# Queries of the second cross-attention by seven block products, around the output projection

## The chip, the cores and the metric

The kernel runs on one NeuronCore of one Trainium2 chip. The metric is the device time of one execution in microseconds (us); a lower time is better. The engines are called PE (TensorE, matrix products; its weight loads are shown as PEld), DVE (VectorE), ACT (ScalarE), POOL (GpSimd) and SP (SyncE, which here only issues transfers).

## The reference, cut to what matters

A decoder of two layers works on 8 sequences of 256 tokens with 256 features, all in float32. Each layer has self-attention, cross-attention and an expert stage, each with a residual sum. The change lies in the cross-attention of the second layer, 16 heads of 64:

```python
q = _split_heads(jnp.einsum('bnd,df->bnf', x, Wq))        # x: 8 x 256 x 256 after a layer norm, Wq: 256 x 1024
kv = jnp.einsum('bmc,cf->bmf', context, Wkv)              # context: 8 x 256 x 512, Wkv: 512 x 2048
k, v = jnp.split(kv, 2, axis=-1)
...                                                        # a null key and value are put in front
sim = jnp.einsum('bhid,bhjd->bhij', q * scale, k)
out = jnp.einsum('bhij,bhjd->bhid', jax.nn.softmax(sim, axis=-1), v)
out = jnp.einsum('bnf,fd->bnd', out, Wout)                 # Wout: 1024 x 256
out = (out - mu) * jax.lax.rsqrt(var + EPS) * ln_scale + ln_bias
```

## The kernel before

The program is traced in Python and then put in order by a planner: for each engine it chooses the order of the instructions by the order of the source and by when its own model of the chip has each one ready. An engine then runs its instructions strictly in that order, and an instruction whose inputs are not ready holds up all behind it. In a region marked `manual_schedule(engines={PE})` the instructions of PE keep the order of the source among themselves; where instructions from outside the region fall between them, and the order on the other engines, stay the planner's.

The stage is `null_cross_attention` (line 1057). It loops over the 8 sequences b (line 1359; called rounds here). A round has these steps:

1. `context(b + 1)` issues the load of the next sequence's context from SP into ctxT (512 KB, two buffers in the pool `ctxs`, line 765).
2. `weighted` (1220): for each of 8 chunks of two heads the scores `stx` from qT and kT, their exponential on ACT (`pTx`), the sum of both key halves on POOL (`both`), the products with the values (`ox`) and the denominators (`den`). In this part PE's order is the planner's.
3. `layernorm_T(b + 1)` (262): the next sequence's rows are normalized on DVE into `xn`, transposed on PE (`tr`, line 283) and copied by ACT into `xnT`. Both tiles have two buffers.
4. `sums_of_context` (1105): four sums of blocks of ctxT on DVE, for step 6.
5. From b = 1 on, `routed_norm(b - 1)` and `routed_rows` (958, 968) do the same as step 3 with the finished rows of sequence b - 1, for the router (tile `xne`, in the buffers of `xn`).
6. From here PE's order is that of the source. Keys and values of sequence b + 1 are made by `seven` (1121): the product of a 2 x 2 block matrix with a 2 x 2 block matrix by seven block products instead of eight. `seven` is a generator, and each `next` makes one step of it:

- step 1: product 1 into bank x; ACT copies the bank (p).
- step 2: product 2 into bank z, and DVE adds p: block (0,0) of the result. Product 5 into bank y; ACT copies it (v).
- step 3: product 6 onto bank x; ACT copies it (u).
- step 4: product 7 onto bank x; DVE adds v: block (1,1).
- step 5: product 3 onto bank y; DVE adds u: block (0,1). Then product 4 onto bank x; ACT copies it: block (1,0).

The first index of a block is the half of the tokens, the second the half of the features. In the program's names the products write `kv` and `kvz`. The sums of weight blocks are made once, ahead of the loop (`sums_of_weights`, 1094).
7. `reciprocals` (1283) of the denominators go through memory (rd, rs on SP) and POOL multiplies them into oT (`divide`, 1315).
8. `routed_scores(b - 1)` (971): the router's scores, small products into `sc`.
9. `queries` (1205): first the null key's scores (`nps`, ACT exponentiates them into `en`), and behind step 10 the queries of sequence b + 1, `fm`, by `feature` (1062): eight products of half a block each, 64 matmul records in 4 PSUM tiles, which DVE copies into qT.
10. `outward` (1321): the output projection `wo`, a copy by ACT, statistics on DVE, a power on POOL, normalized rows on DVE, scale and bias on POOL, and the residual sum on POOL.

The order in which PE gets steps 6, 8, 9 and 10 is written out by hand:

```python
for made in (k7, k7, v7, k7, k7, v7, v7):
    next(made)
if b:
    routed_scores(b - 1)
next(q)
next(v7)
next(v7)
...
divide(oT, rs, (nc.gpsimd, nc.gpsimd if more else nc.vector))
outward(b, oT, old)
if more:
    *_, (qT, en) = q
```

The queries of sequence 0 are made ahead of the loop; the last round makes none. PSUM has three tiles of the kind `mm` (one bank), two of the kind `sc` (two banks: `stx`, and the banks x and y of `seven`) and one for the denominators.

Of the kernel before, what the change touches and what calls it, by code (L numbers as in the profile page):

```python
# [155 lines left out]
def plain(  # L156
# [105 lines left out]
    def layernorm_T(b, work, mm):  # L262

        xn = work.tile([P, 2, D], F32, tag="xn", name="xn")
        mv, rs = norm_stats([x[:, 2 * b + t, :] for t in range(2)], 1e-5, small, "ln")
        for t in range(2):
            last = normed(xn[:, t, :], x[:, 2 * b + t, :], mv, rs, t)
        return last, transposed(xn, work, mm, "xnT")
# [9 lines left out]
    def transposed(rows, work, mm, tag, dst=None):  # L278

        ps = mm.tile([P, 2, 2 * P], F32, tag="mm", name="tr")  # L280
        for t in range(2):
            for c in range(2):
                nc.tensor.transpose(ps[:, c, t * P : (t + 1) * P], rows[:, t, c * P : (c + 1) * P], ident)  # L283
        if dst is None:
            dst = work.tile([P, 2, 2 * P], F32, tag=tag, name=tag)
        nc.scalar.copy(dst, ps)  # L286
        return dst
# [472 lines left out]
    def weights_x():  # L760

        w_exp.close()
        wd = ctx.enter_context(tc.tile_pool(name="wd", bufs=1, side="right"))
        wproj = ExitStack()
        ctxs = wproj.enter_context(tc.tile_pool(name="ctxs", bufs=2, side="right"))
        wp = wproj.enter_context(tc.tile_pool(name="wp", bufs=1, side="right"))
        wkv_x = wp.tile([P, CTX // P, 2 * XH * XD], F32, name="wkv_x")
        wq_x = wp.tile([P, 2, XH * XD], F32, name="wq_x")
        wout_x = wd.tile([P, XH * XD // P, D], F32, name="wout_x")
        nc.gpsimd.dma_start(wkv_x, a["L1_xattn_Wkv"].rearrange("(c p) f -> p c f", p=P))  # L770
        nc.gpsimd.dma_start(wq_x, a["L1_xattn_Wq"].rearrange("(c p) f -> p c f", p=P))
        nc.gpsimd.dma_start(wout_x, a["L1_xattn_Wout"].rearrange("(c p) f -> p c f", p=P))
        nkv = a["L1_xattn_null_kv"]
        nkrow = wd.tile([P, XD], F32, name="nkrow")
        nc.sync.dma_start(nkrow, nkv[0:1, :].to_broadcast([P, XD]))
        nvcol = wd.tile([P, 1], F32, name="nvcol")
        for g in range(2):
            nc.sync.dma_start(nvcol[XD * g : XD * (g + 1), :], nkv[1:2, :].rearrange("o d -> d o"))
        lns = wd.tile([P, D], F32, name="lns")
        nc.sync.dma_start(lns, a["L1_xattn_ln_scale"].rearrange("(o d) -> o d", o=1).to_broadcast([P, D]))  # L780
        lnb = wd.tile([P, D], F32, name="lnb")
        nc.sync.dma_start(lnb, a["L1_xattn_ln_bias"].rearrange("(o d) -> o d", o=1).to_broadcast([P, D]))
        return wd, ctxs, wproj, wkv_x, wq_x, wout_x, nkrow, nvcol, lns, lnb
# [174 lines left out]
    def routed_norm(b, work):  # L958

        xn = work.tile([P, 2, D], F32, tag="xn", name="xne")  # L960
        mv, rs = norm_stats([x[:, 2 * b + t, :] for t in range(2)], 1e-5, small, "ln")
        for kept, v in zip(norms[b], (mv, rs)):
            nc.gpsimd.tensor_copy(kept, v)
        for t in range(2):
            normed(xn[:, t, :], x[:, 2 * b + t, :], mv, rs, t)
        return xn
# [90 lines left out]
    def null_cross_attention(phase):  # L1057
# [4 lines left out]
        def feature(dst, w, rows, copy, c2):  # L1062

            n = w.shape[1]
            ps = mm.tile([P, 2, S], F32, tag="mm", name="fm")
            for i in range(2):
                for cc in range(n):
                    product(ps[:, i, :], w[:, cc, (c2 + i) * P : (c2 + i + 1) * P], rows[:, cc, :], cc == 0, cc == n - 1)
            copy(dst[:, c2 : c2 + 2, :], ps)

        def features(dst, w, rows, copy):
            for c2 in range(0, nc8, 2):
                feature(dst, w, rows, copy, c2)
# [6 lines left out]
        def keys(ctxT):  # L1080
            kT = work.tile([P, nc8, S], F32, tag="kT", name="kTx", bufs=1)
            features(kT, wkv_x, ctxT, nc.scalar.copy)
            return kT

        half = CTX // P // 2

        def w_block(j, k):

            return wkv_x.rearrange("p c (m k f) -> p c m k f", m=2, k=2)[:, half * j : half * (j + 1), :, k, :]

        tw = wsum.tile([P, 3, half, 2, XH * XD // 2], F32, name="tw")
        t1, t2, t3, t4 = tw[:, 0], tw[:, 1], w_block(0, 1), tw[:, 2]

        def sums_of_weights(n):
            dst, p, q = (
                (t1, w_block(0, 1), w_block(0, 0)),
                (t2, w_block(1, 1), t1),
                (t4, w_block(1, 0), t2),
                (t3, w_block(1, 1), w_block(0, 1)),
            )[n]  # L1100
            for m in range(2):
                for c in range(half):
                    nc.vector.tensor_tensor(dst[:, c, m], p[:, c, m], q[:, c, m], ALU.subtract)

        def sums_of_context(ctxT):


            def block(i, j):
                return ctxT[:, half * j : half * (j + 1), bass.ts(i, P)]

            sw = wsum.tile([P, 3, half, P], F32, tag="sw", name="sw")
            s1, s2, s3, s4 = sw[:, 0], sw[:, 1], block(1, 0), sw[:, 2]
# [6 lines left out]
        w_terms = w_block(0, 0), w_block(1, 0), w_block(1, 1), t4, t1, t2, t3  # L1119

        def seven(terms, m, dst):

            xy = scp.tile([P, 2, 2 * S], F32, tag="sc", name=f"kv{m}")
# [8 lines left out]
            def product_of(n, bank, fresh):  # L1132

                s, t = terms[n - 1], w_terms[n - 1][:, :, m, :]
                for i in range(4 if m == 0 else 1):
                    for c in range(half):
                        if m == 0:
                            args = bank[:, bass.ts(i, P)], t[:, c, bass.ts(i, P)], s[:, c, :]
                        else:
                            args = bank, s[:, c, :], t[:, c, :]  # L1140
                        for made in product(*args, fresh and i == 0 and c == 0, c == half - 1):
# [4 lines left out]
            if m == 0:  # L1146
# [7 lines left out]
            else:  # L1154

                def of(i, j):
                    return dst[:, i, 8 * j : 8 * j + 8, :]

                def seen(bank):
                    return bank.rearrange("p (h d) -> p h d", h=8)  # L1160

            def kept(bank, name):
                t = work.tile([P, 2 * S], F32, tag="pT", name=f"kv{name}{m}", bufs=4)
                reads(bank, nc.scalar.copy(t, bank))
                return seen(t)
# [4 lines left out]
            zb = mm.tile([P, 2 * S], F32, tag="mm", name=f"kvz{m}")  # L1170
# [12 lines left out]
            reads(yb, nc.vector.tensor_tensor(of(0, 1), u, seen(yb), ALU.add))  # L1183
            product_of(4, xb, False)
# [3 lines left out]
        def vals(ctxT):  # L1188
            v = work.tile([P, 2, XH, XD], F32, tag="vx", name="vx", bufs=1)
# [13 lines left out]
            return v  # L1203

        def queries(xnT):

# [5 lines left out]
            yield  # L1212
            qT = work.tile([P, nc8, S], F32, tag="qT", name="qTx", bufs=1)
            for c2 in range(0, nc8, 2):
                feature(qT, wq_x, xnT, nc.vector.tensor_copy, c2)
                if c2 == 0:
                    yield
            yield qT, en
# [102 lines left out]
        def outward(b, oT, en):  # L1321
# [9 lines left out]
            for t in range(2):  # L1331
                xt = x[:, 2 * b + t, :]
                normed(y[:, t, :], y[:, t, :], mv, rs, t)
                nc.gpsimd.tensor_tensor(y[:, t, :], y[:, t, :], lns, ALU.mult)
                nc.gpsimd.tensor_tensor(y[:, t, :], y[:, t, :], lnb, ALU.add)
# [11 lines left out]


        _, xnT = layernorm_T(0, work, mm)
        ctxT = context(0)  # L1350
        kT = keys(ctxT)
        for n in range(3):
            sums_of_weights(n)
        v = vals(ctxT)
        *_, (qT, en) = queries(xnT)
        sums_of_weights(3)
        load_router()
        order = ExitStack()
        for b in range(B):
# [4 lines left out]
            if more:  # L1364
                _, xnT = layernorm_T(b + 1, work, mm)
                terms = sums_of_context(ctxT)
# [10 lines left out]
            if more:  # L1377
                order.enter_context(tc.manual_schedule(engines={mybir.EngineType.PE}))
                kT = work.tile([P, nc8, S], F32, tag="kT", name="kTx", bufs=1)
                v = work.tile([P, 2, XH, XD], F32, tag="vx", name="vx", bufs=1)  # L1380
                k7, v7, q = seven(terms, 0, kT), seven(terms, 1, v), queries(xnT)
# [7 lines left out]
            if more:  # L1389

                for made in (k7, k7, v7, k7, k7, v7, v7):
                    next(made)
                if b:
                    routed_scores(b - 1)
                next(q)
                next(v7)
                next(v7)
# [5 lines left out]
            outward(b, oT, old)  # L1403
            if more:
                *_, (qT, en) = q
# [1231 lines left out]
```

## Time and profile before

| | us |
|---|---|
| median of 3 runs | 1377.46 |
| lowest and highest | 1375.84 to 1378.7 |
| the profiled execution | 1375.28 |
| its span in the profile | 1373.6 |

The span reaches from the first to the last instruction that the profile shows; the profiled execution's own time is 1.7 us longer. The granted clock of PE was 0.994 of full speed over the span. The stage of the change runs from 659 to about 1150 us. A float32 product appears in the trace as two records of MATMUL and two of LDWEIGHTS; `product` (272) makes two products of 64 columns each, so it stands for four records. The "mean ns" of a matmul record is its latency; records overlap, so a step is costed from its start to the start of the next.

### The profile page before, as it was taken

What the parts mean: (1) busy time and instruction counts of PE and PEld (TensorE: products, weight loads), DVE (VectorE), ACT (ScalarE), POOL (GpSimd) and SP (SyncE); (2) the same over time, 40 slices, a digit from 0 to 9 for tenths busy, and PEclk for the clock granted to TensorE, in tenths of its full rate; (3) what the DMA queues carried; (4) which work ended last, traced back from release to release, by engine and by line L of the source; (5) the groups of instructions that cost most, each with busy time, mean ns of one, the idle gap of its engine ahead of it and who ended that gap; (6) DMA issues with size and microseconds to landing.
All of it is one profiled execution on the core that took longest, in us unless ns stands there. A gap on an engine that the chain in (4) does not pass through costs nothing.

```text
span 1373.6 us, 30022 instructions
## 1 busy us (share of the span) xinstructions
PE 1333.9 (97%) x12814; PEld 902.7 (66%) x12814; DVE 533.9 (39%) x1539; ACT 457.2 (33%) x730; POOL 404.6 (29%) x513
## 2 busy tenths in 40 slices
PE   6999999999999999999999999999999999999998
PEld 3666756756766756764767566676756645788884
DVE  5443563463475555344233222232232236322223
ACT  2455443543543433531313223131322212022221
POOL 4322052051033243320334424152442512400004
PEclk9999999999999999999999999999999999999999
DMA  8960000000000004100011010101101111689954
GB/s 311 340 224 16 9 25 1 17 24 1 2 9 2 2 9 153 72 2 1 27 36 33 16 32 16 48 6 43 33 1 33 64 32 36 264 336 399 395 196 129
DMA packets 46926, 116.65 MB, mean 85 GB/s; under 512 B 8272, under 2 KB 30400, under 8 KB 42432
## 3 DMA queue, kind: packets, MB, share of 16 engines
q1 hardware_dynamic: 38912, 92.74, 19.7%
q0 software_dynamic: 5152, 18.89, 3.8%
q10 hardware_dynamic: 2720, 3.02, 0.6%
q8 instruction: 103, 1.69, 0.5%
q14 instruction: 39, 0.32, 0.1%
HBM read 104.00 MB, written 27.93 MB: 96 GB/s over the span
## 4 chain that ended last, share of the span: by engine, by line
PE 82%; DMA 6%; DVE 5%; POOL 3%; issue 1%; ACT 1%; SPq 1%; ACTq 0%; POOLq 0%; DVEq 0%
PE kv L274 11%; PE st L334 8%; PE o L366 8%; PE h L274 6%; PE fm L274 5%; PE wo L274 5%; PE ox L1266 4%; PE stx L1228 4%; PE out L1625 3%; PE out L1442 3%; PE h L952 3%; PE qk L274 3%; PE hx L952 3%; PE tr L283 2%; PE den L1242 2%; PE ao L274 2%
## 5 line engine op out<-in xcount | busy, mean ns | idle before, releaser
L366 PE MATMUL o<-pT,padv 128*64 128x256 f32 (+1 forms) x1536 | 171.6, 365 | 1.2 <-POOL pT L346 1.2
L343 ACT ACTIVATE pT<-st 128x1024 f32<-128x1024 f32 (+1 forms) x128 | 110.4, 915 | 88.2 <-PE st L334 87.4
L366 PEld LDWEIGHTS o<-pT,padv 128*64 128x64 f32 x1536 | 103.1, 137 | 52.7 <-issue 9.9
L334 PE MATMUL st<-qm,kT 64*128 64x256 f32 (+1 forms) x1024 | 116.3, 365 | 0.9 <-DVE qm L312 0.6
L334 PEld LDWEIGHTS st<-qm,kT 64*128 64x128 f32 x1024 | 89.2, 188 | 25.9 <-issue 15.6
L1234 POOL TENSOR_TENSOR both<-pTx 128x512 f32<-128x512 f32 x64 | 79.7, 1280 | 55.4 <-ACT pTx L1232 38.9
L1232 ACT ACTIVATE pTx<-stx 128x1024 f32<-128x1024 f32 x64 | 62.1, 1021 | 88.1 <-PE stx L1228 87.6
L274 PE MATMUL h<-xrT,w 128*64 128x128 f32 (+1 forms) x1936 | 87.0, 250 | 1.5 <-issue 1.5
L274 PEld LDWEIGHTS h<-xrT,w 128*64 128x64 f32 x1936 | 84.4, 137 | 4.3 <-issue 2.1
L256 POOL TENSOR_TENSOR lnrs<-lnve,mhalf 128x2 f32<-128x2 f32 x48 | 33.6, 701 | 150.9 <-DVE lnve L254 99.1
L343 ACT ACTIVATE pT<-st,kbias 128x1024 f32<-128x1024 f32 x64 | 68.0, 1113 | 28.7 <-PE st L334 28.7
L334 PE MATMUL st<-qm,memk 64*128 64x256 f32 x512 | 68.8, 393 | 0.5
L945 DVE TENSOR_TENSOR midr<-sl,h 128x128 f32<-128x128 f32 x102 | 29.4, 288 | 102.2 <-PE h L274 69.0
L944 ACT ACTIVATE sl<-h 128x128 f32<-128x128 f32 (+1 forms) x114 | 35.4, 310 | 96.2 <-PE h L274 56.7
L1228 PE MATMUL stx<-qTx,kTx 64*128 64x256 f32 x512 | 64.3, 391 | 2.5 <-ACT pTx L1232 2.5
L346 POOL TENSOR_SCALAR_AFFINE_SELECT pT<-pT 128x512 f32<-128x512 f32 x64 | 39.5, 638 | 83.2 <-ACT pT L343 80.0
L274 PE MATMUL qk<-l_wqkv,xnT 128*64 128x512 f32 x256 | 62.3, 608 | 0.7 <-ACT xnT L286 0.7
L1266 PE MATMUL ox<-pTx,vx 128*64 128x256 f32 x512 | 61.1, 381 | 0.0
L1228 PEld LDWEIGHTS stx<-qTx,kTx 64*128 64x128 f32 x512 | 46.1, 186 | 20.3 <-issue 9.2
L274 PE MATMUL wo<-wout_x,oT 128*64 128x256 f32 x512 | 58.0, 379 | 0.0
L334 PEld LDWEIGHTS st<-qm,memk 64*128 64x128 f32 x512 | 48.0, 186 | 15.1 <-issue 5.1
L274 PE MATMUL fm<-xnT,wq_x 128*64 128x256 f32 x512 | 57.0, 379 | 0.0
(312 smaller groups left out, 2204.2 us busy)
## 6 DMA issues: line engine op xcount, KB each, us to landing
w<-packs SPq DMA_DIRECT2D x22, 1408.0 KB
w<-packs SPq DMA_DIRECT2D x22, 768.0 KB
rs<-rd SPq DMA_DIRECT2D x16, 512.0 KB
packs<-L_ffn_w_eDF SPq DMA_DIRECT2D x8, 704.0 KB
packs<-L_ffn_w_eDF SPq DMA_DIRECT2D x8, 640.0 KB
packs<-L_ffn_w_eFD SPq DMA_DIRECT2D x8, 640.0 KB
ctxT<-ctx_T SPq DMA_DIRECT2D x8, 512.0 KB
wkv_x<-L_xattn_Wkv POOLq DMA_DIRECT2D x1, 4096.0 KB, 18.4
```

The costliest lines, as they stand in the source:

```text
L274: nc.tensor.matmul(out[h], lhsT[:, h], rhs, start=start, stop=stop, skip_group_check=True)
L334: nc.tensor.matmul(st[:, g, i, :n], kT[rows, c, bass.ts(kt, P)], qm[rows, 2 * mq + i, c, q0:], start=True, stop=True,)
L343: nc.scalar.activation(pT[:, :, :, :n], st[:, :, :, :n], AF.Exp, scale=scale, **kb)
L346: nc.gpsimd.affine_select(out=pT[:, :, :, :P], in_=pT[:, :, :, :P], compare_op=ALU.is_ge, fill=0.0, base=0, pattern=[[0, 2], [0, 2], [1, P ...
L366: nc.tensor.matmul(o[64 * i : 64 * i + 64, mq, q0:], v_pad[:, kt, 4 * c + 2 * mq + i, 2 * g : 2 * g + 2, :], pTs[kt][:, g, i, : S - q0], s ...
L952: nc.tensor.matmul(h, shared["ws13"][:, c, lo : lo + P], shared["xnT"][:, c, bass.ts(q, 2 * S)], start=c == 0, stop=c == 1)
L1228: nc.tensor.matmul(st[:, g, kt, :], kT[rows, c, bass.ts(kt, P)], qT[rows, c, :], start=True, stop=True)
L1232: nc.scalar.activation(pT, st, AF.Exp, scale=scale)
L1234: nc.gpsimd.tensor_tensor(both, pT[:, :, 0, :], pT[:, :, 1, :], ALU.add)
L1266: nc.tensor.matmul(o[XD * g : XD * (g + 1), i, :], v[:, kt, 2 * (c2 + i) + g, :], pT[:, g, kt, :], start=kt == 0, stop=kt == 1, skip_group ...
L1442: nc.tensor.matmul(ps, mid[:, i, lo : lo + P], w2[:, i, :], start=i == 0, stop=i == NFC - 1)
L1625: nc.tensor.matmul(ps[h], mid[:, i, h], sets[k % len(sets)][1][:, i, :], start=i == 0, stop=i == NFC - 1, skip_group_check=True,)
```

## The change

The queries, too, are made by `seven`, from xnT (two blocks of 128 features by two blocks of 128 tokens) and wq_x. `seven`, `sums_of_weights` and the sums of rows now take the operands as arguments. For the queries four more sums of weights are made once, and four sums of xnT in each round. The step of products 3 and 4 is cut in two. By the hand-written order products 1, 2, 5 and 6 of the queries stand ahead of the output projection, products 7 and 3, the router's scores, product 4 and the null key behind it. In all rounds but the last, scale and bias of the projected rows move from POOL to DVE. ctxT, xn and xnT have one buffer instead of two in this stage.

```diff
-    def layernorm_T(b, work, mm):
+    def layernorm_T(b, work, mm, bufs=2):
-        xn = work.tile([P, 2, D], F32, tag="xn", name="xn")
+        xn = work.tile([P, 2, D], F32, tag="xn", name="xn", bufs=bufs)
...
-        ctxs = wproj.enter_context(tc.tile_pool(name="ctxs", bufs=2, side="right"))
+        ctxs = wproj.enter_context(tc.tile_pool(name="ctxs", bufs=1, side="right"))
...
-        xn = work.tile([P, 2, D], F32, tag="xn", name="xne")
+        xn = work.tile([P, 2, D], F32, tag="xn", name="xne", bufs=1)
...
+        def w_blocks(w, m, extra):
+            v = w.rearrange("p (j c) (m k f) -> p j c m k f", j=2, m=m, k=2)
+            blocks = [[v[:, j, :, :, k, :] for k in range(2)] for j in range(2)]
+            t1, t2, t4 = (extra[:, i] for i in range(3))
+            return blocks, (t1, t2, blocks[0][1], t4)
...
+        shape = D // P // 2, 1, XH * XD // 2
+        q_blocks = w_blocks(wq_x, 1, wsum.tile([P, 3, *shape], F32, name="twq"))
...
+        def sums_of_rows(rows, n, name, apart):
             def block(i, j):
-                return ctxT[:, half * j : half * (j + 1), bass.ts(i, P)]
+                return rows[:, n * j : n * (j + 1), bass.ts(i, P)]
-            sw = wsum.tile([P, 3, half, P], F32, tag="sw", name="sw")
-            s1, s2, s3, s4 = sw[:, 0], sw[:, 1], block(1, 0), sw[:, 2]
+            sw = wsum.tile([P, 4 if apart else 3, n, P], F32, tag=name, name=name)
+            s1, s2, s4 = (sw[:, i] for i in range(3))
+            s3 = sw[:, 3] if apart else block(1, 0)
...
             product_of(3, yb, False)
             reads(yb, nc.vector.tensor_tensor(of(0, 1), u, seen(yb), ALU.add))
+            yield
             product_of(4, xb, False)
             nc.scalar.copy(of(1, 0), seen(xb))
             yield
...
-        def outward(b, oT, en):
+        def outward(b, oT, en, engine):
...
-                nc.gpsimd.tensor_tensor(y[:, t, :], y[:, t, :], lns, ALU.mult)
-                nc.gpsimd.tensor_tensor(y[:, t, :], y[:, t, :], lnb, ALU.add)
+                engine.tensor_tensor(y[:, t, :], y[:, t, :], lns, ALU.mult)
+                engine.tensor_tensor(y[:, t, :], y[:, t, :], lnb, ALU.add)
                 nc.gpsimd.tensor_tensor(xt, xt, y[:, t, :], ALU.add)
...
             if more:
-                _, xnT = layernorm_T(b + 1, work, mm)
-                terms = sums_of_context(ctxT)
+                _, xnT = layernorm_T(b + 1, work, mm, 1)
+                of_ctx = sums_of_rows(ctxT, CTX // P // 2, "sw", False)
+                of_x = sums_of_rows(xnT, 1, "swq", True)
...
-                k7, v7, q = seven(terms, 0, kT), seven(terms, 1, v), queries(xnT)
+                k7 = seven("k7", of_ctx, w_terms(kv_blocks, 0), kT, False)
+                v7 = seven("v7", of_ctx, w_terms(kv_blocks, 1), v, True)
+                q7 = seven("q7", of_x, w_terms(q_blocks, 0), qT, False)
                 next(k7)
                 rest()
...
-                for made in (k7, k7, v7, k7, k7, v7, v7):
+                for made in (k7, k7, v7, k7, k7, k7, v7, v7, q7, v7, q7, v7, v7, q7):
                     next(made)
-                if b:
-                    routed_scores(b - 1)
-                next(q)
-                next(v7)
-                next(v7)
...
-            outward(b, oT, old)
+            outward(b, oT, old, nc.vector if more else nc.gpsimd)
             if more:
-                *_, (qT, en) = q
+                next(q7), next(q7)
+                if b:
+                    routed_scores(b - 1)
+                next(q7)
+                en = null_key(xnT)
             order.close()
```

`null_key` holds the first half of the former `queries`: the product `nps` and its exponential.

## The prediction

> **What bounds the kernel now.** I read the page's busy table and chain first, then the waits of PE inside the stage that the change touches (659 to 1093 us), then the timelines of PE and of VectorE over one round of its loop. "W" below is the moment in a round at which PE ends the output projection `wo`.
>
> ```profile
> PE 1333.9 (97%) x12814; PEld 902.7 (66%) x12814; DVE 533.9 (39%) x1539; ACT 457.2 (33%) x730; POOL 404.6 (29%) x513
> ...
> PE 82%; DMA 6%; DVE 5%; POOL 3%; issue 1%; ACT 1%; SPq 1%; ACTq 0%; POOLq 0%; DVEq 0%
> ```
>
> PE is the bound, and the chain is PE's. In the touched stage the waits of PE are one kind only, 2.5 us in all: the third score tile of a round waits for the first exponential.
>
> ```profile
> PE stx L1228 <- ACT pTx L1232: 2.5, 8, 0.3
> ```
>
> PE's timeline of the round of b = 1 (start, length, instructions):
>
> ```profile
> 736.65 0.66 PE L283 MATMUL tr<-ident,xn 128*128 128x128 f32 x4
> 737.14 0.60 PE L283 MATMUL tr<-ident,xne 128*128 128x128 f32 x4
> 737.67 1.97 PE L274 MATMUL kv<-ctxT,wkv_x 128*64 128x128 f32 x32
> ...
> 749.04 1.92 PE L274 MATMUL kv<-sw,wkv_x 128*64 128x128 f32 x32
> 750.79 1.92 PE L274 MATMUL kv<-ctxT,tw 128*64 128x128 f32 x32
> ...
> 757.68 0.59 PE L274 MATMUL sc<-router,xnTe 128*64 128x8 f32 x16
> 758.12 1.06 PE L274 MATMUL nps<-xnT,wn 128*64 128x256 f32 x8
> ...
> 771.93 7.08 PE L274 MATMUL fm<-xnT,wq_x 128*64 128x256 f32 x64
> 778.94 2.00 PE L1228 MATMUL stx<-qTx,kTx 64*128 64x256 f32 x16
> ```
>
> Each piece starts where the one before ends, so a step costs start to start. The queries `fm` take 778.94 - 771.93 = 7.01 us. One of the key's block products, 32 records over 128 columns, takes 750.79 - 749.04 = 1.75 us: 54.7 ns a record. A round is 778.94 - 718.55 = 60.39 us. Work saved on PE is time saved, unless a wait takes its place. VectorE at the same W = 771.93:
>
> ```profile
> 772.77 0.75 DVE L251 BATCH_NORM_STATS2 lxst<-yx 128x6 f32<-128x256 f32 x2 [7.95 <-ACT yx L1329]
> 773.44 0.30 DVE L252 BATCH_NORM_AGGREGATE lxmv<-lxst 128x2 f32<-128x6 f32 x2
> 773.77 0.17 DVE L254 TENSOR_SCALAR lxve<-lxmv 128x2 f32<-128x2 f32 x1
> 774.76 0.74 DVE L260 TENSOR_SCALAR yx<-yx,lxmv,lxrs 128x256 f32<-128x256 f32 x2 [0.82 <-POOL lxrs L256]
> 775.41 0.68 DVE L1069 COPY qTx<-fm 128x512 f32<-128x512 f32 x1
> ```
>
> Right behind W VectorE works on the norm of the projected rows, with a hole of 0.82 us in which it waits for GpSimd's power. Today nothing on PE waits for that; in the changed kernel something does.
>
> **The products.** In 7 of 8 rounds the queries become seven products of 16 records over 128 columns, 112 in place of 64 over 256. At 54.7 ns: 6.13 us against 7.01, so 0.88 a round and **6.2 us** in all (a rate of 7/8 exactly). The nearest rows agree, because the key's seven products have this very form. A rule speaks against this: the Trainium skill, "TensorE: Matmul & The Clock Gate", section "Back-to-back issue gap", gives about 81 ns a matmul for a sustained stream of weight loads and matmuls at 128 columns, which would make 112 of them 9.1 us and the change 14 us slower; the row of 1.75 us for 32 denies it here, for these half-width pairs.
>
> **P4 behind P7, the term that decides.** The queries' seven() lays products 1, 2, 5, 6 ahead of `wo`, and 7, 3, the router's scores and 4 behind it. P4 accumulates into the bank that P7 filled, and must wait until VectorE has added that bank into qT. Behind P4 in PE's fixed order stand the null key and the whole next round. PE side: P7 and P3 0.88 each, scores 758.12 - 757.68 = 0.44: PE is ready for P4 at W+2.19 (W+1.75 at b = 0, which has no scores). VectorE side: PE's end to VectorE's start is 0.2 to 0.3 us (750.79 to 751.00, 749.04 to 749.33), the add 0.69, back to PE 0.06. So the add could start at W+1.15, but the norm's instructions stand in VectorE's FIFO. The planner chooses its place:
> - before the norm: P4 at W+1.9; only b = 0 waits, 0.15 us.
> - behind both BATCH_NORM_STATS2 (773.52, W+1.59): P4 at W+2.34; 0.15 x 6 + 0.59 = 1.5 us.
> - behind both aggregates (773.74, W+1.81): P4 at W+2.56; 0.37 x 6 + 0.81 = 3.0 us.
> - behind the epsilon add, in the hole (773.94): P4 at W+2.76; 0.57 x 6 + 1.01 = 4.4 us.
> - behind the normalized rows: see the rivals.
> I take **2.2 us**, between the second and third. Reason: the planner fills the beat between two dependent instructions with an independent one. At the context's sums it issues the sum of line 1116 ahead of that of 1115, which needs the one just issued; an aggregate needs the statistics just issued, and the add is ready by then.
>
> **Smaller waits.** v7's P7 needs ScalarE's copy of P6: 0.28 us to its start, 0.59, 0.06 back (697.66 to 697.94 at b = 0), 0.93; q7's P1 between covers 0.88 where scores and null key covered 1.35: 0.05 x 7 = **0.3 us**. xn has one buffer: xne can be normalized only after xn's transposes. They end at 737.14, VectorE is free at 737.46, both halves end at 738.20, so xne's transposes come 1.1 us later than now. If PE waits, 1.1 x 6 = 6.6 us; if the planner puts the key's first product (1.8 us, no need of xne) ahead, 0. That region of PE's order is the planner's, so I lie near the lower end: 0.1 x 6 = **0.6 us**. qT's last block: P4's copy takes 0.22 + 0.59 + 0.06 = 0.87; the null key behind P4 covers 0.89 (759.01 - 758.12). Cost 0, and up to 0.87 a round without that cover.
>
> **Edits that I cost at nothing.** *ctxT with one buffer*: the load is issued from SP when v7's last product ends, about W - 8.6. Issued at 764.37 its bytes moved until 767.9, so it lands near W - 5; first needed for the sums of the next round's second product, over 20 us on. Only the next round's rd and rs loads stand behind it on SP. If VectorE's order put its sums too early, they would block in a stretch where VectorE is idle (764.8 to 772.77). *ScalarE* gains four copies a round of 0.59; it is busy 33%. *VectorE*: four copies (0.68) become three adds (0.69); four sums of xnT (a 128x128 operation from PSUM took 0.285) and the four scale and bias operations (0.42) are added: +2.2 us a round, mostly behind P4's add. *GpSimd* loses four of 0.73 to 0.75. The skill ("GPSIMD Engine Reference", "Specifications") says that GpSimd shares its SBUF interface with VectorE's two-input instructions; if those eight blocked it outright, that is 2.8 us a round, which GpSimd is spared anyway. *Prologue*: four weight sums of 0.61 to 0.69, in VectorE's holes of 3.9 and 11.2 us before the first scores. *Output projection*: its divide ended at 756.7, `wo` began at 764.16; `wo` moves 2 us later, which only adds slack. *Last round*: unchanged.
>
> **Sum.** The profiled execution took 1375.28 us, a span of 1373.6 and 1.7 around it. -6.2 + 2.2 + 0.3 + 0.6 = -3.1: 1372.2 for it. The median of the runs is 2.2 higher, 1377.5, so 1374.4. What this measurement can tell from no change is about 0.2%, 2.75 us; the forecast lies just beyond.
>
> **Rivals.** *All waits hidden*: the add goes first, or the planner fills PE's hole with the next round's transposes (0.5 us, outside the fixed order): -5.5 to -6.2, 1371.3 to 1372. For it: the hole is only 0.15 to 0.6 us. Against: the norm's instructions are ready first.
> *The gain is eaten*: the add lies in the hole behind the epsilon add and xne's waits are 0.2 a round: -6.2 + 4.4 + 0.3 + 1.2 = -0.3; 1377.2.
> *Slower, VectorE's order*: the add behind the normalized rows (775.50) lets P4 start at W+4.32: 2.13 x 6 + 2.57 = 15.4 us, so +10, 1387.5; behind the four scale and bias operations too (another 1.55, as four such sums took at 763.27), 26 us, +21. For it: in the rows above the planner put a query copy, readable at 773.9, behind the normalized rows, not into the hole. Against: that copy waited for twice the PE work that the add waits for. It decides from an add that starts later than W+2.2: there the wait is the 0.74 us a round that the products leave after the smaller waits. xne's full 1.1 us a round alone would turn the forecast to about +3.
> *The change doesn't save PE time* (54.7 ns doesn't hold with one chunk of contraction): as many ns a column as `wo` or `fm` is 6.13; I see no row for worse.
>
> **How the numbers follow.** Forecast 0.30, all hidden 0.20, eaten 0.25, slower 0.25. The forecast's price is close to the bound, so a part of it counts as no change, and a part of the eaten case as faster: faster 0.46, same 0.28, slower 0.26. Range: down to all hidden, 1371.2, up to nearly the first of the slower cases, 1386.
>
> **What would show it.** Right: 112 records a round on PE at 54.7 ns; a wait of P4 on VectorE of 0.1 to 0.6 us, and the add within 2 us of W. Wrong: that wait at 2 us or more; a wait of `tr` for xne on VectorE near 1 us; a score tile that waits for qT; a round longer than 60.4 us.

## The result, and the profile after

The changed kernel takes 1378.4 us (median of 12 runs, 1375.77 to 1381.23), the kernel before 1377.93 on the same chip (12 runs). The ratio is 1.0002, with a 95% interval of 0.9993 to 1.0012: no change that this measurement can tell. The forecast was 1374.4, in a range of 1371.2 to 1386; the time lies in the range, and the likeliest case did not come. The profiled execution has a span of 1376.4 us against 1373.6 before, at a granted clock of 0.996 against 0.994.

The page of the changed kernel, busy table and chain:

```profile
PE 1336.3 (97%) x13150; PEld 928.6 (67%) x13150; DVE 546.7 (40%) x1592; ACT 474.4 (34%) x758; POOL 384.3 (28%) x485
...
PE 81%; DMA 6%; DVE 5%; POOL 4%; issue 1%; ACT 1%; SPq 1%; ACTq 0%; POOLq 0%; DVEq 0%
```

PE is the bound as before. It has 336 records more (7 x 48, as the products demand) and is busy 2.4 us longer, though the products' work is shorter. So the loss is not idle time. The waits of PE in the stage, 650 to 1090 us, say the same:

```profile
PE stx L1226 <- ACT pTx L1230: 2.5, 8, 0.3
PE q L274 <- DVE qTx L1186: 0.4, 1, 0.4
```

The first was there before. The second is product 4 waiting for the add of product 7 in the round of b = 0. There is no wait of `tr` for `xne`.

PE's timeline of the round of b = 1:

```profile
734.97 0.66 PE L283 MATMUL tr<-ident,xn 128*128 128x128 f32 x4
735.55 0.87 PE L274 MATMUL k<-ctxT,wkv_x 128*64 128x128 f32 x10
736.35 0.44 PE L283 MATMUL tr<-ident,xne 128*128 128x128 f32 x2
736.72 0.44 PE L274 MATMUL k<-ctxT,wkv_x 128*64 128x128 f32 x4
737.09 0.44 PE L283 MATMUL tr<-ident,xne 128*128 128x128 f32 x2
737.46 1.20 PE L274 MATMUL k<-ctxT,wkv_x 128*64 128x128 f32 x17
...
756.60 1.25 PE L274 MATMUL q<-xnT,wq_x 128*64 128x128 f32 x16
757.70 1.94 PE L274 MATMUL v<-wkv_x,ctxT 128*64 128x512 f32 x8
...
773.29 1.92 PE L274 MATMUL q<-swq,wq_x 128*64 128x128 f32 x32
775.04 0.59 PE L274 MATMUL sc<-router,xnTe 128*64 128x8 f32 x16
775.59 1.09 PE L274 MATMUL q<-xnT,twq 128*64 128x128 f32 x16
776.52 1.03 PE L274 MATMUL nps<-xnT,wn 128*64 128x256 f32 x8
777.48 2.00 PE L1226 MATMUL stx<-qTx,kTx 64*128 64x256 f32 x16
```

Two things are to be seen. Behind W = 773.29 stand products 7 and 3 in 1.75 us (54.7 ns a record, as forecast), then scores, product 4 and the null key. And near the start the key's first product is no longer one group of 32 records: the planner has laid the transposes of `xne` into it, in two pairs, after 10 and after 14 of its records. Each pair of transposes, and the four records between the pairs, takes 0.37 us from start to start; four records at 54.7 ns are 0.22, and before the change four transposes took 0.49 (736.65 to 737.14), so two are 0.25. The columns 128*64 and 128*128 (rows by columns of PE in use) show what alternates: products over one half of PE's columns, and transposes over its full width. From `tr` to the first query product this round takes 756.60 - 734.97 = 21.63 us; the same work, from `tr` to the scores, took 757.68 - 736.65 = 21.03 before. That first query product then takes 757.70 - 756.60 = 1.10 us where 16 records are 0.88.

VectorE at the same W:

```profile
774.13 0.76 DVE L251 BATCH_NORM_STATS2 lxst<-yx 128x6 f32<-128x256 f32 x2 [3.64 <-ACT yx L1327]
774.80 0.17 DVE L252 BATCH_NORM_AGGREGATE lxmv<-lxst 128x2 f32<-128x6 f32 x1
774.88 0.66 DVE L1186 TENSOR_TENSOR qTx<-q7v,q 128x512 f32<-128x512 f32 x1
775.45 0.18 DVE L252 BATCH_NORM_AGGREGATE lxmv<-lxst 128x2 f32<-128x6 f32 x1
...
777.10 0.73 DVE L260 TENSOR_SCALAR yx<-yx,lxmv,lxrs 128x256 f32<-128x256 f32 x2 [0.74 <-POOL lxrs L256]
```

The add of product 7 starts at W+1.59, in the beat between the two aggregates, and product 4 at W+2.30.

A round, first score tile to first score tile, is 777.48 - 716.86 = 60.62 us against 60.39; the round of b = 0 is 59.32 against 59.53. Over the seven rounds with queries that is 423.01 against 421.87, +1.14. The last round's own part, up to `wo`, takes 39.54 against 39.20, because its first `den` takes 1.25 us (1088.65 to 1089.90) in place of 0.91 (1088.99 to 1089.90); its weight loads wait for GpSimd. Together that is 1.48 us. The rest of the 2.8 us between the two spans lies outside the stage, and executions of the kernel before alone differ by 5 us (1375.84 to 1380.81).

### The profile page after: what moved, and what is told of

Its sections match the earlier page's. It is cut to its first block, busy times and chain, and to the rows that moved or that the text cites. A ratio compares the mean times of both kernels' runs of the same rounds, so it can differ in the third digit from the quotient of the medians.

```text
span 1376.4 us, 30783 instructions
## 1 busy us (share of the span) xinstructions
PE 1336.3 (97%) x13150; PEld 928.6 (67%) x13150; DVE 546.7 (40%) x1592; ACT 474.4 (34%) x758; POOL 384.3 (28%) x485
## 3 DMA queue, kind: packets, MB, share of 16 engines
q8 instruction: 105, 1.72, 0.5%
## 4 chain that ended last, share of the span: by engine, by line
PE 81%; DMA 6%; DVE 5%; POOL 4%; issue 1%; ACT 1%; SPq 1%; ACTq 0%; POOLq 0%; DVEq 0%
PE st L334 8%; PE o L366 8%; PE v L274 6%; PE h L274 6%; PE k L274 6%; PE wo L274 5%; PE ox L1264 4%; PE stx L1226 4%; PE out L1626 3%; PE out L1443 3%; PE h L952 3%; PE tr L283 3%; PE qk L274 3%; PE hx L952 3%; PE q L274 2%; PE den L1240 2%
## 5 line engine op out<-in xcount | busy, mean ns | idle before, releaser
L1315 POOL TENSOR_TENSOR oT<-oT,rs 128x512 f32<-128x512 f32 x30 | 37.3, 1275 | 64.8 <-DMA rs<-rd 64.8
```

## The experiments

Each kernel is compared with the kernel before on the same chip; the chips differ, and so do the times of the kernel before. Rounds are read from the profiled execution of each kernel.

Theory A: the change gains some 4 us in the products, and the single buffer of `xn` takes it back, because it drives the transposes of `xne` into the key's product. The rival: the wait of product 4 behind VectorE takes it back, as the prediction's rival had it.

**A buffer of its own for `xne`.** It uses the room of the projected rows `y`, free at that time; all else is the changed kernel.

```diff
-        xn = work.tile([P, 2, D], F32, tag="xn", name="xne", bufs=1)
+        xn = work.tile([P, 2, D], F32, tag="y", name="xne", bufs=1)
```

> The changed kernel, but xne gets a buffer of its own (it shares that of y, free at that time), so its transposes need not wait until xn's are done. Theory (the split costs it): PE runs the eight transposes in one piece ahead of the key's first product again; a round falls from 60.62 to about 59.75 us (0.68 at that place and 0.19 behind it, in six rounds), 5.2 us in all, about 1373.2 and some 0.35% under the kernel before. Rival (the gain was lost behind the output projection, at P4): a round stays at 60.6 us, and the time within 1 us of the changed kernel's.

1370.76 us against 1374.99 before, ratio 0.9971 (0.9962 to 0.998). PE's timeline of this kernel:

```profile
735.67 0.66 PE L283 MATMUL tr<-ident,xn 128*128 128x128 f32 x4
736.16 0.60 PE L283 MATMUL tr<-ident,xne 128*128 128x128 f32 x4
736.70 1.97 PE L274 MATMUL k<-ctxT,wkv_x 128*64 128x128 f32 x32
738.49 1.03 PE L1240 MATMUL den<-both,hot 128*64 128x256 f32 x8
```

All eight transposes stand together again and the product is whole. Rounds are 59.82 us, 0.80 shorter than the changed kernel's; 0.80 x 6 = 4.8 us, while the wait of product 4 was left as it was. Theory A holds: this one line is the difference between no change and a gain of 0.3% that can be measured.

**The kernel before, with one buffer for `xn` and `xne` alone.**

```diff
-        xn = work.tile([P, 2, D], F32, tag="xn", name="xne")
+        xn = work.tile([P, 2, D], F32, tag="xn", name="xne", bufs=1)
...
-                _, xnT = layernorm_T(b + 1, work, mm)
+                _, xnT = layernorm_T(b + 1, work, mm, 1)
```

> The kernel before with one buffer for xn and xne in this stage, and nothing else of the change. Theory (the single buffer of xn takes the gain): the transposes are split here too, a round of 60.39 us becomes about 61.25, 5.2 us more in all, 0.38% slower. Rival (the loss comes from the queries' products): a round stays at 60.4 us and the time as before.

1380.43 us against 1374.99, ratio 1.0037 (1.0023 to 1.005). Rounds are 61.20 us, 0.81 longer than before: the same price without any of the queries' products. PE shows the same pattern as the changed kernel, record for record:

```profile
736.59 0.87 PE L274 MATMUL kv<-ctxT,wkv_x 128*64 128x128 f32 x10
737.39 0.44 PE L283 MATMUL tr<-ident,xne 128*128 128x128 f32 x2
737.75 0.44 PE L274 MATMUL kv<-ctxT,wkv_x 128*64 128x128 f32 x4
```

**One buffer, transposes behind `den`.** What costs the time, the passages between the two kinds of matmul, or lateness of `xne`? Here `xne` stays late in the one buffer, but its transposes are written behind the whole first product and the denominators.

```diff
-                routed_rows(b - 1, routed_norm(b - 1, work), work)
+                xne = routed_norm(b - 1, work)
...
                 next(k7)
                 rest()
+                if b:
+                    routed_rows(b - 1, xne, work)
```

> The changed kernel with one buffer for xn and xne, but xne's transposes stand by hand in PE's order behind the key's first product and the last denominators, in one piece, when xne has long been normalized. Theory A (each passage between full-width transposes and half-width products costs 0.17 us): four passages in a round in place of six, none between the two halves of a product: a round of about 60.1 us, 3.2 us less in all. Theory B (PE waits for xne on VectorE and ScalarE): no wait is left, a round of about 59.75 us, 5.2 us less.

1371.74 us against 1374.99, ratio 0.9979 (0.997 to 0.9988); rounds 60.11 us. PE's timeline:

```profile
737.14 1.03 PE L1240 MATMUL den<-both,hot 128*64 128x256 f32 x8
738.11 0.66 PE L283 MATMUL tr<-ident,xne 128*128 128x128 f32 x4
738.69 1.97 PE L274 MATMUL k7z<-ctxT,wkv_x 128*64 128x128 f32 x32
```

Compared with the kernel with a buffer of its own there are two more passages (into the transposes and out of them) and 60.11 - 59.82 = 0.29 us more: 0.15 each. Most of the loss is gone with the buffer still single.

**The pattern by hand, without its cause.** `xne` has its own buffer and is ready early; a hand-written order puts its two pairs of transposes into the first product, once where the planner had put them (after 5 and 7 of its 16 matmuls of 64 columns, two records each, so that one column half has had one more than the other), once after 4 and 6.

```diff
+                                halves.append(nc.tensor.matmul(args[0][h], args[1][:, h], args[2], ...))
+                                if len(read["count"]) + 1 in (5, 7):      # the other kernel: (4, 6)
+                                    next(beside)                          # two transposes of xne
+                                read["count"].append(0)
```

> xne has its own buffer (its rows are normalized early, as in e1), but PE's order is forced to be that of the changed kernel: five products of the key's first block product, two transposes of xne, two products, two transposes, nine products. Theory A (the passages themselves cost): no wait for xne can be left, yet a round takes 60.6 us as in the changed kernel, not 59.82 as in e1. Theory B (PE waited for xne): a round of 59.8 to 59.9 us.

> As e3a, but split after four and six products, so between whole pairs of column halves. Theory (an odd split sets the two column halves off against each other until the projection, 0.19 us): a round of about 60.4 us, and the stretch from the key's products 5 and 6 to the projection as short as in e1 (24.33 us). Rival: the same as e3a.

One run of each: 1379.74 and 1380.28 us, beside 1378.95 for the kernel before; single times cannot part them, so their rounds are compared. The first has rounds of 60.61 us, the changed kernel's to a hundredth, with `xne` ready long before. So nothing waits for `xne`; the pattern itself is the price. PE's timeline of it:

```profile
737.24 0.87 PE L1160 MATMUL k<-ctxT,wkv_x 128*64 128x128 f32 x10
738.04 0.44 PE L1130 MATMUL tr<-ident,xne 128*128 128x128 f32 x2
738.40 0.44 PE L1160 MATMUL k<-ctxT,wkv_x 128*64 128x128 f32 x4
...
758.28 1.25 PE L274 MATMUL q<-xnT,wq_x 128*64 128x128 f32 x16
```

The second, with the even split, has rounds of 60.42:

```profile
738.81 0.66 PE L1160 MATMUL k<-ctxT,wkv_x 128*64 128x128 f32 x8
739.40 0.44 PE L1130 MATMUL tr<-ident,xne 128*128 128x128 f32 x2
739.76 0.44 PE L1160 MATMUL k<-ctxT,wkv_x 128*64 128x128 f32 x4
...
759.86 1.04 PE L274 MATMUL q<-xnT,wq_x 128*64 128x128 f32 x16
```

Four passages cost 60.42 - 59.82 = 0.60, again 0.15 each. The odd split costs another 0.19, and not where it is made: from the key's first product to the query's first both kernels take the same (758.28 - 737.24 = 21.04 us, 759.86 - 738.81 = 21.05). It comes at that query product, whose latency is 1.25 us in place of 1.04. In the kernel before with one buffer the first query work is `fm`, and the odd split shows there: it takes 779.10 - 771.92 = 7.18 us in place of 7.01. The reading that the two column halves run out of step in between fits. With the odd split a product's last record starts behind the first record of the next (`den` at 740.07, the key's last at 740.17); with the even split no record is out of order. The reading was not tried by itself.

**Both waits out.** The buffer of its own, and product 7 of the queries ahead of the output projection, so that product 4 no longer stands close behind its add.

```diff
-                for made in (k7, k7, v7, k7, k7, k7, v7, v7, q7, v7, q7, v7, v7, q7):
+                for made in (k7, k7, v7, k7, k7, k7, v7, v7, q7, v7, q7, v7, q7, v7, q7):
...
                 next(q7), next(q7)
                 if b:
                     routed_scores(b - 1)
-                next(q7)
```

> The changed kernel with a buffer of its own for xne, and with another order by hand: v7's product 4 stands between q7's products 6 and 7, product 7 ahead of the output projection; products 3 and 4, the scores and the null key behind it. Then no product waits for VectorE behind the projection, and scores and null key cover P4's copy. Theory: a round falls to 60.39 - 0.88 = 59.5 us, the full saving of the products; about 6 us under the kernel before, 0.45% faster. Rival (the queries' products themselves are slower than the key's): a round stays above 59.7.

1369.64 us against 1374.99, ratio 0.9965 (0.9953 to 0.9976), below both kernels. Rounds are 59.68 us, not 59.5. In the round of b = 1 PE shows no extra time from W = 772.69 up to the null key:

```profile
772.69 1.04 PE L274 MATMUL q<-swq,wq_x 128*64 128x128 f32 x16
773.57 1.04 PE L274 MATMUL q<-xnT,twq 128*64 128x128 f32 x16
774.44 0.59 PE L274 MATMUL sc<-router,xnTe 128*64 128x8 f32 x16
774.88 1.06 PE L274 MATMUL nps<-xnT,wn 128*64 128x256 f32 x8
775.87 2.00 PE L1226 MATMUL stx<-qTx,kTx 64*128 64x256 f32 x16
```

The null key takes 775.87 - 774.88 = 0.99 to the scores, where it took 0.89 when a product of the values followed it. The score part of the kernel before, which the change doesn't touch, shows the same:

```profile
727.57 1.90 PE L1266 MATMUL ox<-pTx,vx 128*64 128x256 f32 x16
729.39 2.00 PE L1228 MATMUL stx<-qTx,kTx 64*128 64x256 f32 x16
...
732.24 1.90 PE L1266 MATMUL ox<-pTx,vx 128*64 128x256 f32 x16
733.96 1.03 PE L1242 MATMUL den<-both,hot 128*64 128x256 f32 x8
```

Sixteen records of `ox` take 1.82 us when score tiles follow, and 1.72 when `den` follows. So a passage of about 0.1 us leads into the score tiles, and the 7.01 us of `fm` had held it: `wo` runs at 107.9 ns a record (7.77 us for 72), by which 64 records are 6.91. The products therefore save about 0.78 us a round, not 0.88. One wait is new: at b = 0, where no router's scores stand between, the first score tile waits 0.2 us for ScalarE's copy of product 4 into qT.

**Product 4 ahead of product 3**, in the kernel just shown; it was to let the last copy into qT start earlier, in case the 0.1 us ahead of the score tiles is a wait for that copy.

```diff
-            product_of(3, yb, False)
-            reads(yb, nc.vector.tensor_tensor(of(0, 1), u, seen(yb), ALU.add))
-            yield
-            product_of(4, xb, False)
-            nc.scalar.copy(of(1, 0), seen(xb))
+            for which in (4, 3) if four_first else (3, 4):
```

> As e7, and in the queries product 4 comes ahead of product 3, so that ScalarE's copy of product 4 doesn't wait for VectorE's add of product 3. Theory: the first score tile no longer waits for that copy, a round falls from 59.68 to about 59.58 us; 5.5 us under the kernel before, 0.4% faster. Rival (the rest of a tenth lies elsewhere): 59.68 as in e7.

A miss: 1386.46 us against 1378.95, ratio 1.0054 (1.0039 to 1.0069). The waits of PE in its stage:

```profile
PE stx L1228 <- DVE qTx L1191: 9.8, 7, 1.9
```

VectorE in the round of b = 0, where W is 715.47:

```profile
718.31 0.74 DVE L260 TENSOR_SCALAR yx<-yx,lxmv,lxrs 128x256 f32<-128x256 f32 x2 [0.83 <-POOL lxrs L256]
718.96 0.76 DVE L1334 TENSOR_TENSOR yx<-yx,lns 128x256 f32<-128x256 f32 x2
719.63 0.76 DVE L1335 TENSOR_TENSOR yx<-yx,lnb 128x256 f32<-128x256 f32 x2
720.30 0.68 DVE L1191 TENSOR_TENSOR qTx<-q7u,q 128x512 f32<-128x512 f32 x1
```

Product 3's add, one product later than it was, lost its place to normalized rows, scale and bias, and starts at W+4.83. The second score tile waits for it, and from b = 1 on a round takes 61.08 us or more in place of 59.68. That is the prediction's slower rival with another victim. That this tile needs the bank that the add reads, and not its result, is argued from the two tiles of that kind in PSUM and was not tried. The run answers the question of the 0.1 us all the same: at b = 1 the copy ends at 778.24, and the null key still takes 779.75 - 778.75 = 1.00 us to the score tiles. So it is no wait for the copy.

**Product 4's add behind scale and bias.** The changed kernel, with VectorE told to take the add of product 7 only after the last bias.

```diff
-                next(q7), next(q7)
+                with tc.issue_after(last.ins):
+                    next(q7)
+                next(q7)
```

> The changed kernel, but the add of the queries' product 7 is issued on VectorE behind scale and bias of the projected rows. By the prediction's slower rival P4 then starts 5.9 us after the projection's end in place of 2.3: a round of about 64.1 us, and about 25 us more than the changed kernel in all (some 1.8% slower than before). Other theory (the planner's or PE's reordering fills the hole): under 5 us more.

One run: 1413.76 us, 34.8 above the kernel before (1378.95), some 10 more than expected. PE's waits in the stage:

```profile
PE q L274 <- DVE qTx L1186: 19.8, 6, 3.7
```

And three stretches of the round of b = 1, where W is 780.45: the wait, product 4, and the null key. The columns are the stretch, its length, the busy time (and instructions) of PE, PEld, DVE, ACT and POOL, the granted clock, and DMA's share and rate:

```profile
782.20:786.00 3.80, 0.58 (x20) 0.49 (x16) 2.95 (x10) 0.00 (x0) 1.54 (x3) 0.92 0.00 0
786.00:787.76 1.76, 1.76 (x16) 1.76 (x18) 1.76 (x8) 0.00 (x0) 0.62 (x1) 0.50 0.00 0
787.76:789.24 1.48, 1.48 (x12) 0.71 (x9) 0.70 (x6) 0.59 (x1) 1.14 (x4) 0.65 0.00 0
```

Product 4 starts at W+5.55 (5.87 expected), so the order does what was worked out. What was left out is the second line above. In the stretch of 3.8 us PE is busy for 0.58, with the router's scores, and then waits 3.22; behind it the granted clock is 0.50, product 4 takes 1.76 us instead of 0.93, and the null key 1.48 instead of 0.96. That is 1.35 us on top in this round. The Trainium skill, "TensorE: Matmul & The Clock Gate", section "Part 1: The HAM clock gate", has PE fall to half its clock after an idle window of about 3.4 us. The trace agrees in the fall to half; the idle time ahead of it is 3.22 us here, and the next experiment has the same fall behind shorter waits.

**Scale and bias left on GpSimd.**

```diff
-            outward(b, oT, old, nc.vector if more else nc.gpsimd)
+            outward(b, oT, old, nc.gpsimd)
```

> The changed kernel, but scale and bias of the projected rows stay on GpSimd in all rounds. Prediction's theory (this edit costs and brings nothing on PE): rounds of 60.6 us as in the changed kernel. Rival: with only 4.2 us between the projection and the next scores, GpSimd's four operations of 0.73 us hold up the sums of the exponentials and with them the denominators; a round is 0.3 to 1 us longer, with a wait of PE on GpSimd.

One run: 1388.43 us beside 1377.17. Rounds are 61.88 us (61.09 for b = 6), 1.26 longer than the changed kernel's, and the last one up to `wo` is 43.0 in place of 39.5. The waits of PE up to 1090 us, and one row of PE's timeline in the last round:

```profile
PE den L1240 <- POOL both L1232: 5.2, 11, 0.6
```

```profile
1100.08 3.41 PE L1264 MATMUL ox<-pTx,vx 128*64 128x256 f32 x16
```

The projection now ends 4.2 us ahead of the next scores instead of 7.0, so more of GpSimd's work on its rows lies where GpSimd makes the sums for the denominators. In the last round `den` waits 1.24 and 0.63 us, and behind these two waits the granted clock falls to 0.50: this `ox` takes 3.33 us to the next score tiles (1103.41) in place of 1.82. The move to VectorE is no side step of the change; without it the change would cost about 11 us (1388.43 - 1377.17, single runs).

**The kernel before with one buffer for ctxT alone** (`bufs=1` in the pool `ctxs`).

> The kernel before with one buffer for the context in place of two, and nothing else. Prediction's theory (the load is hidden): rounds of 60.4 us as before, no wait of PE on VectorE or on a transfer. Rival: the later sums of the context hold up VectorE, and PE waits for the key's second product or the projection's norm; rounds longer by up to 1 us.

One run: 1376.08 us beside 1377.17. Rounds are 60.39 us, as before, and PE's waits hold nothing new. The later load is hidden.

## Why the prediction was right, and where it was wrong

The time lies in the range, but not because the sum was right: the range reaches from a gain to a loss, two errors of 0.7 us (products and product 4) cancel, and the term of `xne` is off by 4.2 us. Its own signs of being right all came: 112 records at 54.7 ns, a wait of product 4 of 0.1 to 0.6 us, its add within 2 us of W. Of those of being wrong one came: a round longer than 60.4 us. By its own steps, over the seven rounds:

| step | predicted, us | measured, us |
|---|---|---|
| products | -6.2 | about -5.5 |
| product 4 behind product 7 | 2.2 | about 1.5 |
| v7's product 7 | 0.3 | about 0.5 |
| late `xne` | 0.6 | 4.8 |
| sum | -3.1 | +1.3 by the parts, +1.14 by the rounds |

*The products* run at 54.7 ns a record, as the key's did. The saving was 0.1 us a round too high, because the start to start of `fm` contained the passage into the score tiles; this is worked out from the rows above, not measured alone.

*Product 4.* The reason given, that the planner fills the beat between two dependent instructions, was right: the add lies between the aggregates, just behind the statistics. The second case of the four (1.5 us) came, and the value taken between it and the third was a little high. The measured price is the 0.11 us by which the scores' piece is longer (775.59 - 775.04 = 0.55 against 0.44) and the 0.05 of product 4's own, times six, and 0.59 at b = 0 (product 4 starts at W+2.29 where W+1.75 was possible, and takes 0.05 longer). Taking the product apart from its add gained 59.82 - 59.68 = 0.14 a round and 0.34 at b = 0.

*v7's product 7.* In the kernel with a buffer of its own it starts 0.91 us behind the queries' first product, which alone is 0.88, and takes 1.77 us itself in place of 1.72: 0.08 in six rounds. At b = 0 it costs nothing new, because the kernel before had the same wait there. The parts exceed the rounds by some 0.03 a round, by which the null key is shorter where it no longer stands behind the router's scores (0.96 in place of 0.99).

*Late `xne`* is the step that failed. The prediction saw that the single buffer brings the transposes 1.1 us later, and gave two ends: PE waits (6.6 us), or the planner covers the wait with the key's first product (0). It took 0.6, near cover. The planner did cover it, and the cover was the price: it cut the product in three, four passages of 0.15 and an odd split of 0.19 made 0.80 us a round, 4.8 in six. A wait and its cover were not the only two outcomes; filling a hole on an engine can have a cost of its own, and it shows in no list of waits because PE counts as busy. The Trainium skill says in "TensorEngine Tiling (Array Packing)", section "Key Properties", that a change of tiling mode drains the engine; it gives no time. By the columns in the rows the passages measured here are such changes; that draining is what takes the 0.15 us was not tried by itself. The prediction had not asked how many of them the planner's filling would add.

*The rival "the gain is eaten"* gave 1377.2 and lies nearest. Its result came, its mechanism only in part: the add was not in the hole behind the epsilon add, and the `xne` term was four times its 0.2 a round. *The slower rival* did not come in this kernel; the add put last and product 3 put last show that its order can come and that its wait is real (product 4 at W+5.55, summed as 5.87), with more to pay where the clock falls: 34.8 us, summed as 21.

*Edits costed at nothing.* ctxT's buffer and the extra work of VectorE cost nothing in the rounds. The move of scale and bias cost nothing as made, but the prediction did not see that it was needed: it counted GpSimd's relief as a bonus. Of GpSimd's later work one trace remains, the wait of `den` at the start of the last round: +0.34 us in a round called "unchanged". Whether VectorE's added instructions hold up GpSimd, which the prediction allowed for, no run here shows.

## What to carry to other kernels

Where an engine's order is left to a planner, an input that comes later does not only wait or hide: ask which instructions will be put in its place, and count the changes between full-width and half-width matmuls that this makes. Judge PE by start to start of its pieces against records times their rate, because lost time inside a busy group is on no list of waits. Before a buffer is taken away to make room, look for a tile that is idle at that time: sharing the room of `y` gave back 4.8 us.

## What the runs showed of the hardware

- Into the score tiles of 64 rows there is a passage of about 0.1 us too: 16 records of `ox` take 1.82 us ahead of them and 1.72 ahead of `den`; the null key takes 0.99 in place of 0.89.
- Each passage between 128-column transposes and products over 64 columns took 0.15 us (0.29 for two, 0.60 for four).
- An odd number of 64-column matmuls ahead of a full-width one cost 0.19 us, some 20 us later in the round; in the kernel before with one buffer it showed at `fm`, 35 us later.
- The granted clock fell to 0.50 behind a wait of PE of 3.22 us, and the next two products took 3.24 us in place of 1.89. It fell to 0.50 as well behind two waits of 1.24 and 0.63 us with four records between them.
